# A decoder layer on one core: first slab's input first, contexts turned beside the last scan, and the triangles' products behind five of the values' eight stages

## The chip, the cores and the metric

The kernel runs on one core of a Trainium2 chip. Its engines work side by side, each with its own queue of instructions: TensorE (PE, matrix products and transposes; PEld is its weight load), VectorE (DVE), ScalarE (ACT), GpSimd (POOL) and SyncE (SP, which only issues transfers here). ACT issues transfers too, in the same queue as its activations. An engine takes its instructions strictly in the order of its queue and waits at one whose inputs are not there. The metric is the device time of one execution in microseconds (us), lower is better; it is the median of several runs.

## What is computed

One layer over x of shape (4, 1024, 256) in float32: a gated delta-rule attention, a cross attention to a context of shape (4, 77, 256), and a mixture of 8 experts (2 per token). Each is added to its input and layer-normalised. The change touches the first part and the way into the second.

```python
# attention, per head (4 heads, 64 key and 128 value channels)
normed = layernorm(x) * ln_w + ln_b
q, k, v = (causal_conv_silu(normed @ W, conv) for q, k, v)     # 4 taps
beta = sigmoid(normed @ Wb)
g = -exp(A_log) * softplus(normed @ Wa + dt_bias)
for t:                                                         # over 1024 tokens
    S = S * exp(g_t)
    v_eff = (v_t - k_t S) * beta_t
    S = S + k_t^T v_eff
    o_t = q_t S
x = layernorm(2 x + (rms(o) * norm_w * silu(normed @ Wg)) @ Wo)
# cross attention: 16 heads of 64, keys and values from the context
kh, vh = rms(ctx @ Wk), ctx @ Wv
x = layernorm(2 x + softmax(rms(x @ Wq) kh^T, masked by length) vh @ Wo)
# mixture of experts, layernorm
```

## The kernel before

**Tiling.** The 1024 tokens are cut into 8 slabs of 128, each for all 4 batch rows at once. The token-by-token recurrence is done slab by slab: within a slab the triangular system is inverted (first 32 x 32 blocks by a recurrence on DVE, then doubled on PE), between slabs the state S is carried. For one slab i the steps are generators, cut by `yield`:

- `normed(i)` (L303) loads x (L306, on SP's queue), takes the statistics (DVE L310, L311), the scale and offset rs and nm (L195 to L197, the power on POOL), and normalises on ACT (nrm, L316).
- `decays(i)` (L323) turns nrm on PE (L335), applies ln_w and ln_b on ACT (nT, L339), multiplies by Wb and Wa (pb, L352), and computes beta and the log decay g by a polynomial of some twenty small DVE steps (L366 to L388), with two Exps on ACT (L365, L376).
- `cumulated(i)` (L392) sums g over the slab by products with three triangular or full matrices (pd, L397: "the triangles' products"), takes their Exp (ex, L407; every such Exp is noted in the list `exps`) and copies parts of it on DVE (el, qw, L413 to L417).
- `project(i)` (L421) makes keys and queries: product (pp, L287), first tap on ACT (L297), three taps on DVE (L299), Silu (L442), squares (L444), and lengths (L431 to L471). `convolve` (L281) does product and taps for one of 8 channel blocks in two stages.
- `values(i)` (L474) does the same for the 4 value blocks, so 8 stages; `silus` (L478) then applies their Silu (L485), placed on ACT behind every Exp in `exps`, since Exp and Silu need different tables.
- `prepare` (L490), `blocks` (L534: the recurrence on DVE, between transfers through DRAM), `invert` (L579) and `scan` (L638) do the inversion and the recurrence itself. A scan ends with x after the attention, written to DRAM (L797).

**Order.** `interleave` (L221) steps the generators in turn, one step of each per round. For every slab one interleave runs the preparation of slab i+1, the inversion of slab i, and a chain of `decays(i+2)`, `values(i)` and `cumulated(i+2)`. Then come the Silus, and a second interleave with the scan of slab i, the recurrence of slab i+1, the projection of slab i+2 and the input of slab i+3. The start (L828 to L832) does the first slabs' steps in the same way. This written order is a priority: when the program is built, a planner fills each engine's queue from it, and an instruction that it holds to be ready can go ahead of an earlier one that is not.

**The last scan and the contexts.** Before the last scan (L854) the memory of the projection weights is given up (L845) and the cross attention's key weights are loaded into it (xwk, L853). Behind it the contexts are loaded (cx, L880), after them lens, Wv, Wo, Wq and four slabs of x, all on SP. Two zero fills (vz, L965 and L966, one on POOL, one on DVE) and one of the keys' block-diagonal tile (L894, POOL; named wdn in the profile, whose memory it uses) follow, then the contexts are turned on PE (pc, L914) and copied (cT, L917). `keys` (L919: product L924, norm with a power on POOL L939, a factor `alive` from lens L940) and `projected` (L968: values times Wv, L975, then times Wo, L1000) use cT.

**Transfers at the start.** SP's queue has the constants (sq, nw, cols, rows), then the slabs' x. ACT's queue has rw (router), rows of zeros for xd (L169) and xg (L161), Wq, Wk, Wv (L245), wba (L249), wg (L251) and wo (L253). wo is scaled by norm_w on DVE (L259). The largest of them are x (512 KB a slab), xg (1,040 KB), Wq, Wk and Wv (1,024 KB together), wg and wo (512 KB each).

Of the kernel before, what the change touches and what calls it, by code (L numbers as in the profile page):

```python
# [17 lines left out]
P = 128  # L18
# [92 lines left out]
def kernel(ctx: ExitStack, tc: tile.TileContext, a: dict, out: bass.AP):  # L111
# [18 lines left out]

    sq = const.tile([P, NSQ, P], F32, name="sq")
# [9 lines left out]
    nc.scalar.dma_start(out=rw, in_=a["rwT"].rearrange("(c p) e -> p c e", p=P))  # L141
# [19 lines left out]
    nc.scalar.dma_start(  # L161
# [7 lines left out]
    nc.scalar.dma_start(out=xd[NS * B * P :, :], in_=zero[:, 0, 0:D])  # L169

    def tokens(i, src=None):

        if src is None:
            return xd[i * B * P : (i + 1) * B * P, :].rearrange("(b p) d -> p b d", b=B)
        return src[:, i * P : (i + 1) * P, :].rearrange("b p d -> p b d")
# [59 lines left out]
    scan_scope, proj_scope = ExitStack(), ExitStack()  # L235
    wp = scan_scope.enter_context(tc.tile_pool(name="dw", bufs=1))
    wk = scan_scope.enter_context(tc.tile_pool(name="dwk", bufs=2))
    slab = scan_scope.enter_context(tc.tile_pool(name="dslab", bufs=3))
    pj = proj_scope.enter_context(tc.tile_pool(name="pj", bufs=1, side="right"))

    wqkv = pj.tile([P, KC, NCH * P], F32, name="wqkv")
    wba = pj.tile([P, KC, 2 * H], F32, name="wba")
    off = 0
    for name, n in (("L0_attn_Wq", D), ("L0_attn_Wk", D), ("L0_attn_Wv", DV)):
        nc.scalar.dma_start(  # L245
            out=wqkv[:, :, off : off + n], in_=a[name].rearrange("(c p) n -> p c n", p=P)
        )
        off += n
    nc.scalar.dma_start(out=wba, in_=a["wba"].rearrange("(c p) n -> p c n", p=P))  # L249
    wg = wp.tile([P, KC, DV], F32, name="wg")  # L250
    nc.scalar.dma_start(out=wg, in_=a["L0_attn_Wg"].rearrange("(c p) n -> p c n", p=P))  # L251
    wo = wp.tile([P, H, D], F32, name="wo")
    nc.scalar.dma_start(out=wo, in_=a["L0_attn_Wo"].rearrange("(h p) n -> p h n", p=P))  # L253

    pnw = bank("pnw")
    nc.tensor.transpose(pnw[:, 0:P], rows[:, R_NW : R_NW + HV], ident)
    nwc = wp.tile([P, 1], F32, name="nwc")
    nc.vector.tensor_scalar_mul(nwc, pnw[:, 0:1], HV**0.5)
    nc.vector.tensor_scalar_mul(  # L259
        wo.rearrange("p h n -> p (h n)"), wo.rearrange("p h n -> p (h n)"), nwc  # L260
    )


# [39 lines left out]
    def normed(i, made):  # L303

        made["x"] = xi = slab.tile([P, B, D], F32, tag="xi", name="xi", bufs=4)
        nc.sync.dma_start(out=xi, in_=tokens(i, a["x"]))  # L306
        mv = slab.tile([P, B, 2], F32, tag="mva", name="mva")
        for b in range(B):
            st = slab.tile([P, 6], F32, tag="sta", name="sta", bufs=4)
            nc.vector.bn_stats(st, xi[:, b, :])  # L310
            nc.vector.bn_aggr(mv[:, b], st)  # L311
        rs, nm = scales(slab, mv, B, "a")
        nrm = []
        for b in range(B):
            n = pj.tile([P, D], F32, tag="nrm", name="nrm", bufs=4)
            nc.scalar.activation(  # L316
                n, xi[:, b, :], AF.Identity, scale=rs[:, b : b + 1], bias=nm[:, b : b + 1]
            )
# [27 lines left out]


# [73 lines left out]
    def project(i, made):  # L421

        nT, beta, ex = made["nT"], made["beta"], made["ex"]
# [47 lines left out]
        nc.vector.scalar_tensor_tensor(cd, ex[:, 1], -1.0, nb, ALU.mult, ALU.mult)  # L471
# [380 lines left out]

    xload(xwk, "Wk")  # L853
    interleave(*scans(NS - 1))  # L854
# [24 lines left out]
    cx = cp.tile([SC, B, D], F32, name="cx", bufs=1)  # L879
    nc.sync.dma_start(out=cx, in_=a["ctx_1024"].rearrange("b s d -> s b d"))  # L880
# [28 lines left out]

    cT = cp.tile([P, KC, B * SC], F32, name="cT", bufs=1)  # L910
    for c in range(KC):
        pt = bank("pc", "pt")
        for b in range(B):
            nc.tensor.transpose(  # L914
                pt[:, b * SC : (b + 1) * SC], cx[:, b, c * P : (c + 1) * P], ident[:SC, :SC]
            )
        nc.vector.tensor_copy(cT[:, c, :], pt[:, 0 : B * SC])  # L917
# [743 lines left out]
```

## Time and profile before

| | us |
|---|---|
| three runs | 1768.39, 1771.73, 1775.53 |
| median | 1771.73 |
| the profiled execution's own time | 1777.84 |
| its span, first to last instruction | 1776.1 |
| PE busy | 1589.0 (89%) |
| DVE busy | 1177.7 (66%) |
| ACT busy | 935.8 (53%) |
| POOL busy | 565.8 (32%) |
| mean granted TensorE clock | 0.945 of full |

The profiled execution is one more run beside the three; what lies outside its span is 1.7 us. A line of the timeline gives start and duration in us, engine, line of the kernel, operation, the tile written and the tiles read, the shape, the number of instructions, and in brackets how long the engine had been idle and what ended that. The stages of the span, with the busy times of PE and DVE in each:

| stretch, us | what runs | PE busy | DVE busy |
|---|---|---|---|
| 0 to 115 | first inputs, first keys, first inversion | 53.90 | 62.76 |
| 115 to 207 | one slab: inversion, then scan | 87.51 | 68.16 |
| 207 to 298 | the next | 85.27 | 69.42 |
| 745 to 806 | last values, last scan | 52.87 | 28.03 |
| 806 to 888 | contexts, keys, values of the cross attention | 61.48 | 38.77 |
| 888 to 1330 | cross attention | 428.35 | 349.15 |
| 1330 to 1776 | experts | 403.57 | 230.58 |

### The profile page before, as it was taken

Reading aid. Unit: us, or ns where it says so; the run is one execution under the profiler, and the core shown is the slowest. Engines: PE = TensorE matmul, PEld = TensorE weight load, DVE = VectorE, ACT = ScalarE, POOL = GpSimd, SP = SyncE. Lnnn points to the kernel's source line nnn. Section 1 sums busy time; section 2 is a strip of 40 time slices with the busy share of each in tenths; the row PEclk is TensorE's granted clock in tenths of the full one; section 3 lists DMA queues with packets and bytes.
Section 4 is the critical chain, followed back from the end, with each engine's and each line's share of the span. In section 5 each row is a group of like instructions: output and inputs, shape, how many; then the busy total and the mean of one; then the engine's idle time right before and its main releaser. Section 6 shows DMA issues by size and latency. Waiting matters only on the chain. (4 is left out here: it accounts for less than half of the span.)

```text
span 1776.1 us, 28454 instructions
## 1 busy us (share of the span) xinstructions
PE 1589.0 (89%) x9524; PEld 1152.4 (65%) x9524; DVE 1177.7 (66%) x3557; ACT 935.8 (53%) x2214; POOL 565.8 (32%) x486
## 2 busy tenths in 40 slices
PE   4658999999989998985889999999989999999991
PEld 3246777676767766762657777887765666666660
DVE  4658686877777776735456888888865655555554
ACT  3425555555556454551278888888743333333333
POOL 2311312121212112014045666666733322222222
PEclk9869999898989898998999999999999999999995
DMA  4010101010101010103050011111263322332226
GB/s 142 18 19 22 39 19 43 19 43 19 43 19 30 19 31 19 25 31 132 0 190 13 22 46 43 37 49 37 94 216 67 69 45 46 46 48 46 45 33 199
DMA packets 119023, 94.20 MB, mean 53 GB/s; under 512 B 56939, under 2 KB 108639, under 8 KB 118367
## 3 DMA queue, kind: packets, MB, share of 16 engines
q1 hardware_dynamic: 100127, 69.14, 13.6%
q0 software_dynamic: 13296, 17.83, 6.0%
q10 hardware_dynamic: 5456, 5.41, 0.9%
q8 instruction: 78, 1.28, 0.3%
q14 instruction: 66, 0.54, 0.1%
HBM read 55.46 MB, written 36.90 MB: 52 GB/s over the span
## 5 line engine op out<-in xcount | busy, mean ns | idle before, releaser
L1536 POOL DMA_INDIRECT xd<-my,mrow x71 | 110.6, 1557 | 294.4 <-ACT my L1535 268.7
L1105 ACT ACTIVATE sc<-sc,ntop,rq 128x77 f32<-128x77 f32 x512 | 182.4, 448 | 5.2 <-DVE ntop L1100 4.6
L1136 PE MATMUL pxo<-ball,aT 128*128 128x256 f32 (+1 forms) x640 | 151.4, 384 | 0.8 <-DVE xs L1147 0.8
L287 PE MATMUL pp<-nT,wqkv 128*128 128x262 f32 x512 | 149.1, 430 | 0.2 <-PE pu L620 0.2
L1066 POOL TENSOR_TENSOR rq<-rq,nhalf 128x8 f32<-128x8 f32 x64 | 106.8, 1669 | 129.2 <-DVE rq L1065 128.1
L1487 PE MATMUL pgt<-wall,mxT 128*128 x284 | 134.6, 596 | 0.5 <-ACT mxT L1420 0.5
L1487 PE MATMUL pup<-wall,mxT 128*128 x284 | 134.4, 596 | 0.0
L1514 PE MATMUL pdn<-wdn,mhT 128*128 x568 | 134.2, 379 | 0.0
L759 POOL TENSOR_TENSOR so<-so,nhalf 128x4 f32<-128x4 f32 x32 | 32.6, 1018 | 312.3 <-DVE so L758 312.3
L1136 PEld LDWEIGHTS pxo<-ball,aT 128*128 128x128 f32 (+1 forms) x640 | 118.0, 192 | 15.1 <-DVE xs L1147 1.4
L1049 PE MATMUL pq<-wdn,xT 128*128 128x512 f32 x256 | 120.6, 594 | 1.5 <-ACT qsq L1059 1.0
L299 DVE SCALAR_TENSOR_TENSOR kq<-pp,cols,kq 128x256 f32<-128x256 f32 x192 | 88.3, 478 | 38.9 <-ACT kq L297 36.3
L287 PEld LDWEIGHTS pp<-nT,wqkv 128*128 128x128 f32 x512 | 99.6, 209 | 21.8 <-issue 3.3
L1514 PEld LDWEIGHTS pdn<-wdn,mhT 128*128 128x128 f32 x568 | 102.5, 190 | 11.0
L1495 DVE TENSOR_TENSOR sge<-pgt,ball 128x512 f32<-128x512 f32 x71 | 49.1, 692 | 85.3 <-PE pgt L1487 84.4
L1496 ACT ACTIVATE sge<-sge 128x512 f32<-128x512 f32 x71 | 44.7, 630 | 111.8 <-DVE sge L1495 111.8
L1487 PEld LDWEIGHTS pup<-wall,mxT 128*128 128x128 f32 x284 | 54.5, 192 | 69.0 <-issue 69.0
L1497 DVE TENSOR_TENSOR pup<-pup,ball 128x512 f32<-128x512 f32 x71 | 49.7, 699 | 69.8 <-PE pup L1487 69.7
L1114 POOL TENSOR_TENSOR sc<-sc,den 128x616 f32<-128x616 f32 x64 | 78.2, 1221 | 55.0 <-DVE den L1113 41.0
L1535 ACT ACTIVATE my<-my,mw 128x256 f32<-128x256 f32 x71 | 36.1, 508 | 106.3 <-DVE my L1534 106.3
L299 DVE SCALAR_TENSOR_TENSOR v<-pp,cols,v 128x256 f32<-128x256 f32 x192 | 81.6, 476 | 13.9 <-ACT v L297 13.2
L1085 PE MATMUL psc<-wdn,qT 128*128 128x154 f32 x512 | 78.7, 295 | 7.2 <-ACT qT L1077 7.2
(313 smaller groups left out, 3693.9 us busy)
## 6 DMA issues: line engine op xcount, KB each, us to landing
mx<-xg SPq DMA_DIRECT2D x71, 130.0 KB, 2.1
xs<-xd SPq DMA_DIRECT2D x12, 512.0 KB, 9.5
xi<-in_x SPq DMA_DIRECT2D x8, 512.0 KB, 5.1
am<-ab SPq DMA_DIRECT2D x16, 256.0 KB, 3.7
xd<-kd SPq DMA_DIRECT2D x32, 128.0 KB, 1.7
wall<-in_L_ffn_gate_w SPq DMA_DIRECT2D x8, 512.0 KB, 9.6
wall<-in_L_ffn_up_w SPq DMA_DIRECT2D x8, 512.0 KB, 8.6
xd<-xs SPq DMA_DIRECT2D x8, 512.0 KB, 4.8
```

Source lines behind the costliest of these rows:

```text
L287: mm(pp[:, 0 : 2 * (HALO + P)], lhsT=wqkv[:, kc, c * P : (c + 1) * P], rhs=nT[:, kc, 2 * j : 2 * j + 2, :].rearrange("p b t -> p (b t)"), ...
L299: nc.vector.scalar_tensor_tensor(ch, pre[:, :, n : n + P], cols[:, w0 + n : w0 + n + 1], ch, ALU.mult, ALU.add)
L1049: mm(pq, lhsT=t["xT"][:, kc, :], rhs=xwq[:, kc, c0 : c0 + HH * XD], start=kc == 0, stop=kc == KC - 1,)
L1066: nc.gpsimd.tensor_tensor(rq, rq, nhalf[:, :HH], ALU.pow)
L1085: mm(ps[:, c * 2 * SC : (c + 1) * 2 * SC], lhsT=qT[:, 2 * g + c, :], rhs=kbd[:, b, half * XC // 2 + 2 * g + c, :], start=True, stop=True,)
L1105: nc.scalar.activation(sc[:, h], sc[:, h], AF.Exp, scale=t["rq"][:, h : h + 1], bias=t["ntop"][:, h : h + 1])
L1114: nc.gpsimd.tensor_tensor(sc, sc, bc(den.unsqueeze(2), [P, HH, SC]), ALU.mult)
L1136: mm(px[:, 0:D], lhsT=aT[:w, c, :], rhs=vo[:w, b, half * NV + c, :], start=half == 0 and c == 0, stop=half == 1 and c == NV - 1,)
L1487: mm(ps, lhsT=t["xT"][:, c, :], rhs=wall[:, bass.ds(e * EW + off + c * FF, FF)], start=c == 0, stop=c == KC - 1,)
L1497: nc.vector.tensor_tensor(pu, pu, ball[:, bass.ds(e * FF + B_U, FF)], ALU.add)
L1514: mm(px[:, 0:D], lhsT=t["hT"][:, f, :], rhs=wdn[:, bass.ds(e * EV + f * D, D)], start=f == 0, stop=f == FC - 1,)
L1536: nc.gpsimd.indirect_dma_start(out=xd, out_offset=bass.IndirectOffsetOnAxis(ap=row, axis=0), in_=y, in_offset=None, compute_op=ALU.add,)
```

## The change

It has five parts.

1. x of slab 0 is loaded by the first instruction on SP's queue (`slab_of_x`), ahead of the constants. On ACT's queue only Wq, Wk, Wv and wba are left, now at its head. rw, the two fills with zeros, wg and wo move to SP's queue; wg, wo and the scaling of wo are written behind `normed(0)`.
2. `decays` has one more `yield`, between nT and the product pb.
3. At the start, `cumulated(0)` is put behind the first five stages of `project(0)` instead of ahead of it; `project` reads `ex` only where it uses it.
4. In each slab's first interleave, `cumulated(i+2)` is put behind five of the eight stages of `values(i)` instead of behind all of them.
5. The contexts' tiles cx and cT move into the pool of xwk; cx is loaded ahead of xwk, before the last scan, and the contexts are turned and copied by a third generator beside the two of the last scan.

```diff
+    def slab_of_x(i):
+        xi = slab.tile([P, B, D], F32, tag="xi", name="xi", bufs=4)
+        nc.sync.dma_start(out=xi, in_=a["x"][:, i * P : (i + 1) * P, :].rearrange("b p d -> p b d"))
+        return xi
+    x0 = slab_of_x(0)
+    wqkv = pj.tile([P, KC, NCH * P], F32, name="wqkv")
...
-    nc.scalar.dma_start(out=rw, in_=a["rwT"].rearrange("(c p) e -> p c e", p=P))
+    nc.sync.dma_start(out=rw, in_=a["rwT"].rearrange("(c p) e -> p c e", p=P))
...
-    nc.scalar.dma_start(
+    nc.sync.dma_start(
         out=xg[NE * STRIDE :, :].rearrange("(r p) d -> p r d", p=P), in_=bc(zero, [P, NE, DX])
     )
...
-    nc.scalar.dma_start(out=xd[NS * B * P :, :], in_=zero[:, 0, 0:D])
+    nc.sync.dma_start(out=xd[NS * B * P :, :], in_=zero[:, 0, 0:D])
...
-        made["x"] = xi = slab.tile([P, B, D], F32, tag="xi", name="xi", bufs=4)
-        nc.sync.dma_start(out=xi, in_=tokens(i, a["x"]))
+        made["x"] = xi = slab_of_x(i) if i else x0
...
+        yield
 
         pb = bank("pb")
...
-        nT, beta, ex = made["nT"], made["beta"], made["ex"]
+        nT, beta = made["nT"], made["beta"]
...
-        nc.vector.scalar_tensor_tensor(cd, ex[:, 1], -1.0, nb, ALU.mult, ALU.mult)
+        nc.vector.scalar_tensor_tensor(cd, made["ex"][:, 1], -1.0, nb, ALU.mult, ALU.mult)
...
     interleave(*some(normed, 0, 0))
+    wg = wp.tile([P, KC, DV], F32, name="wg")
+    nc.sync.dma_start(out=wg, in_=a["L0_attn_Wg"].rearrange("(c p) n -> p c n", p=P))
+    wo = wp.tile([P, H, D], F32, name="wo")
+    nc.sync.dma_start(out=wo, in_=a["L0_attn_Wo"].rearrange("(h p) n -> p h n", p=P))
...
-    interleave(chain(*some(cumulated, 0), *some(project, 0, 0)), *some(decays, 1, 1))
+    keys0 = project(0, made[0])
+    interleave(chain(islice(keys0, 5), *some(cumulated, 0), keys0), *some(decays, 1, 1))
...
+        vals = values(made[i])
         interleave(
             *ahead,
             *inverts(i),
-            chain(*some(decays, i + 2, i + 2), values(made[i]), *some(cumulated, i + 2)),
+            chain(*some(decays, i + 2, i + 2), islice(vals, 5), *some(cumulated, i + 2), vals),
         )
...
+    cx = xkv.tile([SC, B, D], F32, name="cx")
+    nc.sync.dma_start(out=cx, in_=a["ctx_1024"].rearrange("b s d -> s b d"))
     xload(xwk, "Wk")
-    interleave(*scans(NS - 1))
+    cT = xkv.tile([P, KC, B * SC], F32, name="cT")
+
+    def contexts():
+        for c in range(KC):
+            pt = bank("pc")
+            for b in range(B):
+                nc.tensor.transpose(
+                    pt[:, b * SC : (b + 1) * SC], cx[:, b, c * P : (c + 1) * P], ident[:SC, :SC]
+                )
+            nc.vector.tensor_copy(cT[:, c, :], pt[:, 0 : B * SC])
+            yield
+
+    interleave(*scans(NS - 1), contexts())
```

(`cx`, its load, `cT` and the same loop are taken out behind the scan.)

More of the change, by code (lines that the diff above doesn't have):

```diff
@@ L128, in new_banks @@
         ps_pool[0] = banks.enter_context(tc.tile_pool(name=name, bufs=bufs, space=PSUM, **kw))
+    scan_scope, proj_scope = ExitStack(), ExitStack()
+    wp = scan_scope.enter_context(tc.tile_pool(name="dw", bufs=1))
+    wk = scan_scope.enter_context(tc.tile_pool(name="dwk", bufs=2))
+    slab = scan_scope.enter_context(tc.tile_pool(name="dslab", bufs=3))
+    pj = proj_scope.enter_context(tc.tile_pool(name="pj", bufs=1, side="right"))
+    def slab_of_x(i):
[4 more added lines that the diff above has]
+    wqkv = pj.tile([P, KC, NCH * P], F32, name="wqkv")
+    wba = pj.tile([P, KC, 2 * H], F32, name="wba")
+    off = 0
+    for name, n in (("L0_attn_Wq", D), ("L0_attn_Wk", D), ("L0_attn_Wv", DV)):
+        nc.scalar.dma_start(
+            out=wqkv[:, :, off : off + n], in_=a[name].rearrange("(c p) n -> p c n", p=P)
+        )
+        off += n
+    nc.scalar.dma_start(out=wba, in_=a["wba"].rearrange("(c p) n -> p c n", p=P))
     sq = const.tile([P, NSQ, P], F32, name="sq")
@@ L168, with tokens @@
     xd = tc.dram_tile([NS * B * P + P, D], F32, name="xd")
-    nc.scalar.dma_start(out=xd[NS * B * P :, :], in_=zero[:, 0, 0:D])
[L171 to L175, printed above, removed]
+    nc.sync.dma_start(out=xd[NS * B * P :, :], in_=zero[:, 0, 0:D])
+    def tokens(i):
+        return xd[i * B * P : (i + 1) * B * P, :].rearrange("(b p) d -> p b d", b=B)
     def rsqrt(pool, src, n, eps, scale, name):
@@ L227, in interleave @@
                     gens.remove(g)
[L235 to L261, printed above, removed]
     nega = pj.tile([P, H], F32, name="nega")
@@ L828 @@
     interleave(*some(normed, 0, 0))
+    wg = wp.tile([P, KC, DV], F32, name="wg")
+    nc.sync.dma_start(out=wg, in_=a["L0_attn_Wg"].rearrange("(c p) n -> p c n", p=P))
+    wo = wp.tile([P, H, D], F32, name="wo")
+    nc.sync.dma_start(out=wo, in_=a["L0_attn_Wo"].rearrange("(h p) n -> p h n", p=P))
+    pnw = bank("pnw")
+    nc.tensor.transpose(pnw[:, 0:P], rows[:, R_NW : R_NW + HV], ident)
+    nwc = wp.tile([P, 1], F32, name="nwc")
+    nc.vector.tensor_scalar_mul(nwc, pnw[:, 0:1], HV**0.5)
+    nc.vector.tensor_scalar_mul(
+        wo.rearrange("p h n -> p (h n)"), wo.rearrange("p h n -> p (h n)"), nwc
+    )
     interleave(*some(decays, 0, 0), *some(normed, 1, 1))
-    interleave(chain(*some(cumulated, 0), *some(project, 0, 0)), *some(decays, 1, 1))
+    keys0 = project(0, made[0])
+    interleave(chain(islice(keys0, 5), *some(cumulated, 0), keys0), *some(decays, 1, 1))
     interleave(*prepares(0), *some(cumulated, 1), *some(normed, 2, 2))
@@ L851, in xload @@
         nc.sync.dma_start(out=w, in_=a[f"L0_xattn_{n}"].rearrange("(c p) n -> p c n", p=P))
+    cx = xkv.tile([SC, B, D], F32, name="cx")
+    nc.sync.dma_start(out=cx, in_=a["ctx_1024"].rearrange("b s d -> s b d"))
     xload(xwk, "Wk")
-    interleave(*scans(NS - 1))
+    cT = xkv.tile([P, KC, B * SC], F32, name="cT")
[5 more added lines that the diff above has]
+                    pt[:, b * SC : (b + 1) * SC], cx[:, b, c * P : (c + 1) * P], ident[:SC, :SC]
+                )
+            nc.vector.tensor_copy(cT[:, c, :], pt[:, 0 : B * SC])
+            yield
+    interleave(*scans(NS - 1), contexts())
     scan_scope.close()
@@ L878 @@
     xwo = cp.tile([P, XC, D], F32, name="xwo", bufs=1)
-    cx = cp.tile([SC, B, D], F32, name="cx", bufs=1)
-    nc.sync.dma_start(out=cx, in_=a["ctx_1024"].rearrange("b s d -> s b d"))
     leni = xk.tile([P, B], I32, name="leni")
@@ L908 @@
     nc.vector.tensor_tensor(wqk, cols[:, C_XQ : C_XQ + 1], cols[:, C_XK : C_XK + 1], ALU.mult)
[L910 to L917, printed above, removed]
     def keys(b):
```

## The prediction

> **What bounds the kernel now.** I read the page's slices first: PE is busy 89% of the span, but the low slices are the first three and slices 19 and 20, the only places where the change moves much. Three questions follow: what starts PE, what PE waits for between two slabs, and what stands between the last scan and the cross attention. Times below are us from the span's start.
>
> The timeline of the first 45 us (start, duration, engine, line; in brackets the idle time before and what ended it):
>
> ```profile
> 10.61 0.75 DVE L310 BATCH_NORM_STATS2 sta<-xi 128x6 f32<-128x256 f32 x2 [3.80 <-DMA xi<-in_x]
> 13.93 0.15 DVE L195 TENSOR_SCALAR rs<-mva 128x4 f32<-128x4 f32 x1
> 13.98 1.28 ACT L265 ACT_TABLE_LOAD   x1 [13.98 <-DMA xi<-in_x]
> 18.02 0.23 DVE L197 SCALAR_TENSOR_TENSOR nm<-mva,rs 128x4 f32<-128x4 f32 x2
> 18.21 4.04 ACT L316 ACTIVATE nrm<-xi,nm,rs 128x256 f32<-128x256 f32 x8 [2.73 <-DVE nm L197]
> 22.97 3.82 PE L352 MATMUL pb<-wba,nT 128*128 128x8 f32 x16 [1.95 <-ACT nT L339]
> 31.15 1.46 PE L397 MATMUL pd<-g,sq 128*128 128x16 f32 x6 [4.36 <-DVE g L388]
> 33.34 1.95 PE L287 MATMUL pp<-nT,wqkv 128*128 128x262 f32 x4
> 35.84 1.52 DVE L299 SCALAR_TENSOR_TENSOR kq<-pp,cols,kq 128x256 f32<-128x256 f32 x3 [2.16 <-ACT kq L297]
> ```
>
> Slab 0's input lands at 10.6. Its scale (rs, 13.93) is followed by its offset (nm) only at 18.02, because DVE has the statistics of slabs 1 and 2 in between and waits for their inputs. Then the key products (L287) stand behind the triangles' product (L397), which waits 4.36 for the polynomial of g. From there one chain runs to the first inversion, and the waits show that PE has nothing else meanwhile:
>
> ```profile
> PE pw L587 <- DMA tt<-ub: 24.3, 1, 24.3
> ```
>
> So what starts this chain earlier starts everything earlier.
>
> Between the last scan and the keys, timeline again:
>
> ```profile
> 806.83 0.70 SPq L880 DMA_DIRECT2D cx<-in_ctx  x1
> 811.14 1.26 PE L914 MATMUL pc<-sq,cx 77*128 77x77 f32 x8 [7.90 <-DMA cx<-in_ctx]
> 814.73 5.34 PE L924 MATMUL pkv<-xwk,cT 128*77 128x512 f32 x8 [2.32 <-DVE cT L917]
> 820.02 1.64 POOL L939 TENSOR_TENSOR kr<-kr,nhalf 77x8 f32<-77x8 f32 x1 [6.70 <-DVE kr L938]
> ```
>
> PE ends the scan at 803.24, waits 7.90 for the contexts and 2.32 for their copies.
>
> Between two slabs (slab 2's values to its scan), ACT and PE:
>
> ```profile
> 324.52 1.28 ACT L485 ACT_TABLE_LOAD   x1
> 326.50 0.40 PE L650 MATMUL pv<-sq,v 128*128 128x128 f32 x1 [1.76 <-ACT v L485]
> 330.40 0.47 ACT L297 ACTIVATE kq<-pp,cols 128x256 f32<-128x256 f32 x1 [2.92 <-PE pp L287]
> 330.78 0.62 ACT L485 ACTIVATE v<-v 128x512 f32<-128x512 f32 x1
> 331.45 0.44 PE L650 MATMUL pv<-sq,v 128*128 128x128 f32 x2 [1.08 <-ACT v L485]
> ```
>
> The Exp of L407 (324.29) has to precede the Silu table and v's Silus. But DVE's 18 convolution steps end only at 328.45 (321.32 + 7.13), so the last Silu cannot come earlier than that.
>
> **The change, part by part.**
>
> *Input first.* x0 is SP's first issue (0.73). The row of four xi loads has 6.3 to 11.5 from issue to landing, the 320 KB of sq 3.4; x0 lands between 0.73 + 3.4 = 4.1 and 7.0, I take 5.5. Statistics 1.75 (10.61 to 12.36), rs 0.15, the power on POOL 1.05, nm 0.2, gaps 0.4: nrm starts at 9.0 against 18.21. Only four nrm now stand before nT (2.0 of the 4.04), so nT ends near 12.7 against 23.58, and pb near 16.5. ACT hid nothing before: its first work (13.98) came just after its last DMA issue (13.58 + 0.37). With five issues fewer it is free by 7.8 (wba's issue, 7.39 + 0.4). Those five (rw, 1,040 KB of xg, xd, wg, wo) go to SP, some 0.45 each = 2.3, all ahead of x1. Bytes ahead of x1's end: 3.7 MB without xg, 5.0 with it; at the 0.37 MB/us of 4 to 20 us, after first bytes at 2.3, x1 lands at 12.4 to 15.8 (before: 13.6). Its statistics and offset take 3.5, so slab 1's transposes, which PE has in order behind the first key product, can run at 16 to 19.5. That costs 0 to 1.1 there and is covered by DVE's backlog. The scaling of wo (0.74, DVE) is now written ahead of slab 1; if it stands before nm of slab 0 it holds the chain until wo lands, some 6.
>
> *Key products before the triangles.* They follow pb at 16.5 instead of 33.34, DVE's steps 2.5 later at 19. Before, these ran 35.84 to 50.37 = 14.5, slab 1's polynomial included. Now slab 0's polynomial (21 steps of 0.17, 3.5), slab 2's statistics (1.75) and el/qw (0.8) share DVE: 20.6, end 39.6 against 50.37, a gain of 10.8. The Exp of slab 0 and the Silus of its keys now mix on ACT: I count two more table loads. The row prices one at 1.28 and the next activation starts 1.31 after the one before (48.87 to 50.18), so 2.6 in all; as ACT has slack in part, I take 1. Start: **-10**; ends -14.5 (no sharing) and -4 (wo in front).
>
> [...]
>
> *Contexts beside the last scan.* Eight transposes (1.26 on PE) and two copies (0.85 on DVE) go into a scan where PE waits anyway (1.91 at 758.31). cx goes out before xwk, whose issue at 754.44 waited 13.7 for PE's last key/value product; with cx's 4.3 (806.83 to 811.1) it lands at 758.7, about when PE asks. Cost 0, at most 1.3 + 1. The keys' first product can then start at 804 to 806.4 instead of 814.73. What is late next is POOL: two memsets end at 813.33 (809.12 + 4.21), and the first power (820.02) can come no earlier than 813.4; alive (813.62 on DVE) is due there too. So 820.02 - 813.4 = 6.6, the rest of the section follows this chain until PE fills at 856. I take **-6**; ends -10.7 (all PE idle) and -3 (xwv, landing near 812 to 816, holds the values' products).
>
> *Triangles behind five stages; a yield before pb.* pd moves ahead of three stages (0.74 of PE, neutral), Exp and Silu table (1.5) into ACT's gaps of 0.41 to 2.53. The 1.76 wait goes, but DVE ends at 328.45 as before, and el/qw (0.75) now stand before its last steps. Per slab, six slabs: -2 (1.76 plus part of the 2.3 that the last Silu stood behind kq) to +0.75. As DVE decides, I take -0.5: **-3**, ends -12 and +4.5.
>
> Sum: -10 - 6 - 3 = -19. Span 1776.1 gives 1757; the profiled run itself took 1777.84, 1.7 more, and the median 1771.73 is 6.1 below that: 1777.8 - 19 - 6.1 = **1753**.
>
> **Rivals.**
> *B, the gains are taken back at once*: wo's scaling or slab 1's input holds the start (-4), the memsets and xwv the keys (-2 to -3), the slabs give 0. Sum -6: 1766. For it: 2.3 of issues and 1.5 MB more before x1 on SP. Against: DVE has nm ready before wo can land, if it is placed so.
>
> *C, slower: PE waits for g.* pb is now written one round later, behind L629. PE's order in the trace is the written one (pk, pu, pb, pl, pp). If it stays so, PE's gap before pl grows from 2.0 (304.11) to 4, and g, from za at 304.4 to 317.72, comes 5.3 later, 323. pd then stands at PE's head from 320.8 (323.52 less three stages of 0.9), with three stages and all the scan's products queued behind: 2.2. The stretch after the present gap shows what idling does besides:
>
> ```profile
> 304.00:310.00 6.00, 5.89 (x37) 5.33 (x38) 2.56 (x13) 2.24 (x6) 1.80 (x2) 0.50 0.00 0
> ```
>
> (after the length stand five engines' busy times, then the granted clock: 0.50). L629 took 3.67 against 2.04 at 672.76, L500 behind it 3.55 against 1.88 at 293.08: 3.3 for the gap of today. For one twice as long I add between nothing and 2.3; with the 2.2 that is up to 4.5 a slab, six slabs 27, less 16 from the rest: 1772 + 11 = 1783. It decides from 2.7 a slab on. Against: pb is ready while PE is idle there, so it need not stay behind.
>
> [...] This trace shows 0.50 after 2.0 already.
>
> *D, ACT decides between the slabs*: both waits (1.76, 1.08) and the 0.88 before L671 go, -2.5 a slab: -15 instead of -3, 1741.
>
> *That it does nothing* would need the x0 issue and the cx issue to stay where they are; both are first in their queue by the text.
>
> **Chances.** Forecast 0.55 (own range 1741 to 1763), B 0.20, C 0.12, D 0.13. With three runs from 1768 to 1776, about 0.5% (9 us) can be told from no change. Faster by more: 0.51 + 0.13 + 0.06 of B = 0.70; within: 0.18; slower: 0.12. The range 1735 to 1775 takes in D's half, the forecast and B, and leaves out C.
>
> **What would show it.** Right: nrm near 9, first L287 near 17, pw L587 near 98 instead of 108.5; PE's pkv at 804 to 807 and kr near 813.4 counted from the scan's end; pd before the last three stages with no wait above 0.5. Wrong: L259 waiting for wo before L197; PE pd waiting for g in each slab; clock 0.5 stretches longer than now; v's last step more than 12 after the first of bp's second eight (317.80 to 328.45 now).

## The result and the profile after

Five runs of the changed kernel took 1781.55, 1789.19, 1789.68, 1791.23 and 1793.37 us, median **1789.68**; five of the kernel before had a median of 1772.98. The ratio is 1.0086, 95% interval 1.006 to 1.0112: slower by 0.9%, where 1753 was forecast with a range up to 1775. The profiled execution is the lowest of the five (1781.55, span 1779.8, granted clock 0.942); the other four had clocks of 0.931 to 0.934.

Read stage by stage in the two profiled executions:

| stretch | before | after | difference |
|---|---|---|---|
| start to the first pw (first inversion) | 108.5 | 101.5 | -7.0 |
| first pw to the last slab's pw | 628.6 | 639.5 | +10.9 |
| last slab's pw to the end of the last scan's px | 66.1 | 68.3 | +2.2 |
| end of the last scan to the first query product | 84.4 | 80.6 | -3.8 |
| from there to the end | 888.5 | 889.9 | +1.4 |

The rows add up to +3.7, and the medians differ by 16.7: the profiled execution before lies 4.9 above its median, the one after 8.1 below. The other runs left no trace, so where the ones after lost their further time is not shown.

The start and the handoff gained, as forecast, though less. The slabs lost as much as these two gained, even in this quickest of the five executions.

**Slabs.** PE's waits (what for; us in total, times, longest us), before, then after:

```profile
PE pl L629 <- DVE tr L623: 8.5, 5, 2.1
```

```profile
PE pl L623 <- DVE tr L617: 20.8, 7, 4.0
PE pv L644 <- ACT v L479: 13.7, 16, 1.7
```

and PE's timeline in slab 3, before (first pw at 384.7) and after (first pw at 379.9):

```profile
397.13 2.73 PE L629 MATMUL pl<-tr,bp 64*64 64x64 f32 x32 [1.66 <-DVE tr L623]
399.79 2.11 PE L287 MATMUL pp<-nT,wqkv 128*128 128x262 f32 x4
```

```profile
392.32 3.64 PE L623 MATMUL pl<-tr,bp 64*64 64x64 f32 x32 [3.51 <-DVE tr L617]
395.89 3.58 PE L346 MATMUL pb<-wba,nT 128*128 128x8 f32 x16
...
399.32 3.76 PE L494 MATMUL pe<-ee,sq 128*128 128x512 f32 x4
403.01 3.67 PE L628 MATMUL pu<-tt,wt 64*64 64x64 f32 x32
406.62 2.11 PE L281 MATMUL pp<-nT,wqkv 128*128 128x262 f32 x4
408.66 3.54 PE L508 MATMUL pk<-kq 64*128 64x256 f32 x16
412.13 3.80 PE L281 MATMUL pp<-nT,wqkv 128*128 128x262 f32 x16
```

pb now stands behind pl, in the place that pp had, so PE has nothing for 3.51 us ahead of pl. Then it works at half speed from pl through pk: pb takes 3.58 (1.95 with the clock full), pu 3.67 (2.08), pk 3.54 (2.00). The same in the windows of this slab (length; busy us of PE, PEld, DVE, ACT and POOL with instructions; then granted clock, DMA share, GB/s):

```profile
379.90:389.90 10.00, 8.90 (x205) 6.94 (x203) 6.44 (x22) 6.78 (x11) 3.46 (x4) 1.00 0.27 80
389.90:399.90 10.00, 7.58 (x49) 7.40 (x50) 4.15 (x13) 2.28 (x6) 3.09 (x3) 0.57 0.01 2
399.90:409.90 10.00, 10.00 (x46) 6.41 (x46) 6.20 (x20) 3.52 (x8) 2.54 (x2) 0.50 0.00 0
409.90:419.90 10.00, 9.79 (x50) 7.88 (x48) 9.47 (x31) 4.45 (x9) 2.08 (x2) 0.90 0.24 33
```

The third line is the one to read: PE is busy all of it, at half clock. A look at busy shares alone would call that stretch perfect.

**Start.** DVE after:

```profile
10.14 0.16 DVE L220 SCALAR_TENSOR_TENSOR nm<-mva,rs 128x4 f32<-128x4 f32 x1
16.88 0.75 DVE L832 TENSOR_SCALAR wo<-wo,nwc 128x1024 f32<-128x1024 f32 x1 [6.59 <-DMA wo<-in_L_attn_Wo]
18.31 0.75 DVE L303 BATCH_NORM_STATS2 sta<-xi 128x6 f32<-128x256 f32 x2 [0.68 <-DMA xi<-in_x]
...
42.53 0.48 DVE L293 SCALAR_TENSOR_TENSOR kq<-pp,cols,kq 128x256 f32<-128x256 f32 x1
```

nm of slab 0 is out at 10.14 in place of 18.02, ahead of the scaling of wo, as forecast. DVE then waits 6.59 for wo, and slab 1's input comes at 18.3 (expected 12.4 to 15.8). The last line is DVE's last convolution step of slab 0's keys: it ends at 43.0, where 39.6 was forecast and 50.4 measured before. From there on the chain is about as long as it was, and the first pw comes 7.0 earlier. ACT loads tables at 30.23, 32.17 and 34.32, where Exp and Silu of two slabs now mix; up to the first pw it has eight loads, six before, which are the two more that were counted.

**Last scan and handoff**, after, PE first (the ACT line between stands beside the first stop):

```profile
762.09 0.46 PE L872 MATMUL pc<-sq,cx 77*128 77x77 f32 x4 [1.86 <-DMA cx<-in_ctx]
...
765.45 0.78 PE L872 MATMUL pc<-sq,cx 77*128 77x77 f32 x4
766.80 1.44 PE L692 MATMUL py<-vt,tt 128*128 128x128 f32 x5 [0.57 <-DVE cT L875]
```

```profile
761.46 0.63 ACT L479 ACTIVATE v<-v 128x512 f32<-128x512 f32 x1 [1.72 <-DVE v L293]
```

```profile
810.13 3.66 PE L937 MATMUL pkv<-xwk,cT 128*77 128x512 f32 x8 [0.81 <-DVE kd L784]
818.50 2.39 PE L988 MATMUL pvt<-cT,xwv 128*128 128x308 f32 x4 [4.71 <-DMA xwv<-in_L_xattn_Wv]
```

The handoff on POOL and on DVE:

```profile
815.21 4.21 POOL L916 MEMSET wdn<- 128x4928 f32 x1
820.52 3.25 POOL L952 TENSOR_TENSOR kr<-kr,nhalf 77x8 f32<-77x8 f32 x2 [1.11 <-DVE kr L951]
```

```profile
815.89 3.54 DVE L921 CAST lens<-leni 128x4 f32<-128x4 int32 x1
815.90 3.53 DVE L949 TENSOR_REDUCE ks<-ksq 77x8 f32<-77x512 f32 x1
```

In the last scan PE's queue stops 1.86 at pc, put down to cx. This stop isn't new: the values that the next product (pv) needs come from ACT at 762.09 as well (761.46 + 0.63), and before PE waited 1.91 for them at the same place. New are the transposes themselves, 0.57 for their copy ahead of py, and a longer spell at half clock behind them: 6.83 us, 3.41 before. The keys' first product starts 0.8 after the scan and not 11.5, but 7 of these 10.7 us are given back: a cast of 512 numbers takes 3.54 and a sum 3.53 (the next sum takes 0.68), both ending with POOL's fill. The first power comes at 820.52, which is 11.2 behind the scan's end (16.8 before), and POOL takes the second power ahead of the first product with `alive`.

### The profile page after: what moved, and what is told of

Its sections match the earlier page's. It is cut to its first block, busy times and chain, and to the rows that moved or that the text cites. A ratio compares the mean times of both kernels' runs of the same rounds, so it can differ in the third digit from the quotient of the medians.

```text
span 1779.8 us, 28453 instructions
## 1 busy us (share of the span) xinstructions
PE 1597.8 (90%) x9524; PEld 1155.6 (65%) x9524; DVE 1177.8 (66%) x3557; ACT 937.3 (53%) x2216; POOL 565.7 (32%) x486
## 5 line engine op out<-in xcount | busy, mean ns | idle before, releaser
L281 PE MATMUL pp<-nT,wqkv 128*128 128x262 f32 x512 | 139.9, 410 | 0.3 <-PE pu L614 0.2
L1149 PEld LDWEIGHTS pxo<-ball,aT 128*128 128x128 f32 (+1 forms) x640 | 118.1, 193 | 15.8 <-DVE xs L1160 2.1
L281 PEld LDWEIGHTS pp<-nT,wqkv 128*128 128x128 f32 x512 | 94.5, 198 | 21.6 <-issue 5.1
L293 DVE SCALAR_TENSOR_TENSOR kq<-pp,cols,kq 128x256 f32<-128x256 f32 x192 | 88.5, 480 | 25.5 <-ACT kq L291 24.1
```

Source lines behind the costliest of these rows:

```text
L281: mm(pp[:, 0 : 2 * (HALO + P)], lhsT=wqkv[:, kc, c * P : (c + 1) * P], rhs=nT[:, kc, 2 * j : 2 * j + 2, :].rearrange("p b t -> p (b t)"), ...
L293: nc.vector.scalar_tensor_tensor(ch, pre[:, :, n : n + P], cols[:, w0 + n : w0 + n + 1], ch, ALU.mult, ALU.add)
L1149: mm(px[:, 0:D], lhsT=aT[:w, c, :], rhs=vo[:w, b, half * NV + c, :], start=half == 0 and c == 0, stop=half == 1 and c == NV - 1,)
```

## The experiments

The theories: **T1**, the extra stage of `decays` puts pb behind pl, and PE's idling with the half clock after it costs the slabs (later cut into T1a, the idling as such, and T1b, the later chain of g on DVE); **T2**, the triangles' products behind five stages cost it; **T3**, the transfers on SP or the contexts do. A fourth came up on the way: **T4**, the clock goes by how wide the products are that stand about pl.

### One part undone or alone

`e1_no_yield`: the change without the `yield` between nT and pb.

```diff
-        yield
 
         pb = bank("pb")
```

> The whole change but for its second part: nT and pb stand in one stage of decays again. T1 (the extra stage puts pb behind the products pl, PE then idles up to 4.0 us ahead of pl where it idled 2.1, and the half clock that follows costs the slabs their time): pb is back ahead of pl in PE's queue, PE's longest wait for tr is 2.1 again (20.8 us of waits in all becomes 8 to 9), and the time is 1757 to 1766, below before. T2 (the triangles' products behind five stages cost the slabs their time): 1784 to 1792, as with the whole change. T3 (the transfers moved to SP and the contexts in the last scan cost it): 1784 to 1792 too.

Measured: 1757.89, ratio to before 0.9886 (0.9859 to 0.9913). Waits for tr 8.0.

`e2_no_triangles`: the change with the order of before for `cumulated`.

```diff
-            chain(*some(decays, i + 2, i + 2), islice(vals, 5), *some(cumulated, i + 2), vals),
+            chain(*some(decays, i + 2, i + 2), vals, *some(cumulated, i + 2)),
```

> The whole change but for its fourth part: cumulated stands behind all eight stages of values again. T1: PE still idles 3.5 to 4.0 ahead of pl; the time stays at 1784 to 1794. T2: the slabs are as before, and start and handoff keep their gain of 7.0 + 3.8 - 2.2 = 8.6: 1760 to 1767. T3: 1784 to 1792.

Measured: 1793.15, 1.0087 (1.0061 to 1.0112). The whole change has 1.0086: beside the stage, the triangles' move is worth next to nothing.

`e3_yield_alone`: the kernel before with the `yield`.

```diff
+        yield
         pb = bank("pb")
```

> The kernel before with the second part alone, the stage between nT and pb. T1: PE's longest wait for tr grows from 2.1 to 3 to 4 us, the stretch from the first pw to the last grows by 10 to 20, and the time is 1783 to 1797. T2 and T3: within 4 us of before, 1769 to 1777.

Measured: 1800.35, 1.0134 (1.0107 to 1.016), above T1's 1783 to 1797. Waits for tr 21.0, longest 4.0.

`e4_triangles_alone`: the kernel before with `cumulated` behind five of the eight stages.

```diff
-            chain(*some(decays, i + 2, i + 2), values(made[i]), *some(cumulated, i + 2)),
+            chain(*some(decays, i + 2, i + 2), islice(vals, 5), *some(cumulated, i + 2), vals),
```

> The kernel before with the fourth part alone, cumulated behind five of the eight stages. T1: waits for tr as before (8.5 us in all), the time within 5 us of before, 1767 to 1777. T2: 1783 to 1797, the loss being in the inversions of slabs 3 and 4 above all. T3: within 4 us of before.

Measured: 1759.76, 0.9905 (0.9878 to 0.9932), below what any theory had.

T2 and T3 are out. The one line `yield` costs 22.8 us alone (1800.35 against 1777.59) and 31.8 within the change (1789.68 against 1757.89; the kernel before took 1772.98 beside the one and 1777.59 beside the other, so by the ratios it is 35). T1 had no room for the other half of the result: the triangles' move, without the stage, gains 17.8, and it was priced at 3.

Where it goes is read from one window over six slabs, first pw to seventh pw, in which each kernel has the same 4092 or 4093 products (e6, e8, e9 and e10 have some added). Before, e4, e5 (below: the stage at the start only) and after:

```profile
108.50:659.60 551.10, 517.22 (x4092) 391.72 (x4093) 412.20 (x1366) 308.10 (x714) 114.35 (x110) 0.92 0.13 28
```

```profile
108.20:640.50 532.30, 503.42 (x4093) 381.37 (x4094) 410.90 (x1366) 306.72 (x714) 114.35 (x110) 0.95 0.13 28
```

```profile
103.30:636.20 532.90, 503.88 (x4092) 380.76 (x4093) 411.76 (x1366) 306.79 (x714) 114.28 (x110) 0.95 0.13 29
```

```profile
101.50:664.00 562.50, 522.14 (x4093) 394.74 (x4094) 416.17 (x1366) 306.64 (x714) 114.40 (x110) 0.92 0.12 27
```

The same products keep PE busy for 503.4, 503.9, 517.2 or 522.1 us. That difference is the clock. Adding up the trace's records of the granted clock gives the time at half clock, and an account that holds for all runs: busy time less half of the half-clock time is 473 to 481 where no product is added.

| kernel | six slabs | PE not busy | PE busy | at half clock |
|---|---|---|---|---|
| before | 551.1 | 33.9 | 517.2 | 85.0 |
| e1, no stage | 532.4 | 29.4 | 503.0 | 50.5 |
| e2, triangles as before | 573.0 | 39.4 | 533.7 | 121.9 |
| e3, stage alone | 568.2 | 41.7 | 526.5 | 105.8 |
| e4, triangles alone | 532.3 | 28.9 | 503.4 | 50.4 |
| e5, stage at the start only | 532.9 | 29.0 | 503.9 | 50.9 |
| after | 562.5 | 40.4 | 522.1 | 88.5 |
| e6, unread pb ahead too | 564.1 | 28.0 | 536.1 | 95.0 |
| e7, x1 and x2 first | 533.5 | 27.9 | 505.6 | 55.1 |
| e8, pb twice ahead | 535.3 | 22.1 | 513.2 | 47.2 |
| e9, wide behind pb | 574.7 | 38.7 | 536.1 | 102.4 |
| e10, wide ahead of pb | 532.7 | 26.7 | 506.0 | 34.4 |
| e11, pp ahead of pb | 550.5 | 37.6 | 512.9 | 64.8 |
| e12, pp beside pb | 547.2 | 32.7 | 514.5 | 68.2 |
| e13, as e12 in the slabs | 539.3 | 33.1 | 506.2 | 50.7 |
| e14, as e5 in the slabs | 532.4 | 28.6 | 503.8 | 51.2 |

So from e5 to after the slabs lose 29.6: 11.4 idle and 18.2 clock. From before to e4 they gain 18.8: 5.0 idle and 13.8 clock. That clock is gained at the head of the scan, where PE waits for v: spells of half clock that begin more than 25 us behind a slab's first pw add up to 41.0 us before and to 10.2 in e4. In slab 3 PE waits there 1.76, 1.08 and 0.88 before, and in e4 once:

```profile
414.48 0.44 PE L650 MATMUL pv<-sq,v 128*128 128x128 f32 x2 [1.58 <-ACT v L485]
```

### Where the stage helps

`e5_yield_start_only`: the stage for slabs 0 and 1 alone.

```diff
-        yield
-
+        if i < 2:
+            yield
         pb = bank("pb")
```

> The whole change, with the extra stage of decays for slabs 0 and 1 only. T1 (in the slabs the stage costs time, at the start it helps: the first inversion began at 101.5 with it and at 107.3 without): first pw at 101 to 102, the slabs as without the stage (611 from the first pw to the last), 1749 to 1755. If the stage's place at the start only moved a table load that is paid elsewhere: 1756 to 1760, as without it.

Measured: 1754.84, 0.9888 (0.9864 to 0.9912); first pw at 103.3, six slabs as in e1. The upper end of what was expected: its start is 4.0 better than e1's 107.3, the time 3.1, and by the ratios nothing (0.9888 and 0.9886), so a gain in time from the stage at the start is not shown. Against before the start gains 5.2 here and 7.0 in the whole change, with the same code there.

`e7_x1_x2_first`: e5, and the inputs of slabs 1 and 2 ahead of rw, xg, xd, wg and wo on SP, wo's scaling later.

```diff
+    ahead_x = {0: x0, 1: slab_of_x(1), 2: slab_of_x(2)}
     rw = const.tile([P, KC, NE], F32, name="rw")
...
-    wg = wp.tile([P, KC, DV], F32, name="wg")
...
+    wg = wp.tile([P, KC, DV], F32, name="wg")
...
     interleave(blocks(0, made[0]), *some(project, 1, 1))
```

> As the whole change with the stage for slabs 0 and 1 only, and the inputs of slabs 1 and 2 loaded straight behind the constants, wg, wo and the scaling of wo written behind the preparation of slab 0. If the start is held by slab 1's input, which came at 18.3 behind 2.6 MB on SP's queue, and by DVE's wait for wo: x1 is there at 13 to 15, the first pw comes at 95 to 99, and the time is 3 to 6 below the same kernel without this. If DVE's own backlog holds it: pw within 1.5 of 101.5 and the same time.

Measured: 1758.65, 0.9906 (0.9884 to 0.9927), first pw at 104.9. Missed. DVE's wait for wo is gone and slab 1's statistics are early, but they and slab 2's now stand ahead of slab 0's offset, as in the kernel before. DVE, then ACT:

```profile
14.39 0.23 DVE L221 SCALAR_TENSOR_TENSOR nm<-mva,rs 128x4 f32<-128x4 f32 x2
```

```profile
14.58 4.04 ACT L310 ACTIVATE nrm<-xi,nm,rs 128x256 f32<-128x256 f32 x8 [4.95 <-DVE nm L221]
```

So nm of slab 0 comes at 14.39 (10.36 in e5) and the first key product at 19.78 (14.47), 5.3 later, while the first pw is only 1.6 later than in e5. The run undoes one gain while it makes another, and so it does not show whether the 6.59 us and slab 1's 18.3 were on the path. That stays open.

### Is it the idling?

`e6_pb_twice_behind`: the change, with the product of pb made a first time ahead of the stage, unread.

```diff
+        if i >= 2:
+            pw = bank("pbx")
+            for b in range(B):
+                for kc in range(KC):
+                    mm(pw[:, b * 2 * H : (b + 1) * 2 * H], lhsT=nT[:, kc, b, HALO:], rhs=wba[:, kc, :], ...)
         yield
 
         pb = bank("pb")
```

> The whole change, and for slabs 2 to 7 the product of pb is made once more ahead of the extra stage, into a bank that nothing reads: PE has 1.95 us more of work a slab where it idles ahead of pl, while the pb that g is made from stays behind pl, as in the whole change. T1a (what costs is PE idling 4 us and the half clock after it): waits for tr 8 to 10 us in all, the granted clock 0.945 or more, 1762 to 1772: six slabs pay 1.95 each for the product that stands outside the gap, and no more. T1b (what costs is that g's chain on DVE runs later): 1783 to 1793, no better than the whole change or worse.

Measured: 1784.79, 1.0046 (1.0028 to 1.0063). T1a falls as it was put: the idle time is that of e5 (28.0 against 29.0), the waits for tr 8.4, and yet 95.0 us run at half clock. The time lies in T1b's range; e11 below speaks against T1b. Its slab 3, PE:

```profile
392.28 3.67 PE L634 MATMUL pl<-tr,bp 64*64 64x64 f32 x32 [1.49 <-DVE tr L628]
395.88 3.58 PE L357 MATMUL pb<-wba,nT 128*128 128x8 f32 x16
399.31 3.76 PE L505 MATMUL pe<-ee,sq 128*128 128x512 f32 x4
403.00 3.67 PE L639 MATMUL pu<-tt,wt 64*64 64x64 f32 x32
```

The same stretch of e5, with a gap about as long:

```profile
384.72 2.41 PE L623 MATMUL pl<-tr,bp 64*64 64x64 f32 x32 [1.31 <-DVE tr L617]
387.06 2.11 PE L281 MATMUL pp<-nT,wqkv 128*128 128x262 f32 x4
388.97 2.25 PE L494 MATMUL pe<-ee,sq 128*128 128x512 f32 x4
391.15 2.08 PE L628 MATMUL pu<-tt,wt 64*64 64x64 f32 x32
```

In e5 pp and pe, 262 and 512 columns wide, stand side by side and the clock comes back within pe. In e6 pb, 8 columns wide, stands in pp's place; pe alone is followed by pu, and the half clock goes on for 20.5 us. That is T4.

`e8_pb_twice_ahead`: e5 with the unread pb ahead of the read one, both ahead of pl.

```diff
+        if i >= 2:
+            pw = bank("pbx")
+            ...
         if i < 2:
             yield
         pb = bank("pb")
```

> As the whole change with the stage for slabs 0 and 1 only, and for slabs 2 to 7 the product of pb made twice, both ahead of pl, the first unread: 1.95 us of useless work a slab in the gap ahead of pl that is 1.0 to 2.0 long. T1a (the idling is paid by a half clock behind it): PE's waits for tr nearly 0, the granted clock higher, and the time 4 to 15 below the same kernel without the useless product. T1b, or a clock that doesn't mind gaps under 2 us: 0 to 6 above it.

Measured: 1760.2, 0.9916 (0.9893 to 0.9939): T1a's 4 to 15 below e5 missed, 5.4 above, as the other expectation had it. Two windows of its slab 3 (from its first pw at 371.5) show why:

```profile
371.50:381.50 10.00, 10.00 (x215) 8.07 (x214) 6.60 (x22) 6.77 (x11) 3.48 (x4) 1.00 0.27 82
381.50:391.50 10.00, 10.00 (x64) 7.70 (x63) 6.87 (x26) 4.06 (x10) 3.24 (x4) 0.68 0.00 0
```

PE is busy for all 20 us, and the clock falls all the same, at 385.0. The products of the 5.8 us ahead of the fall have 8 to 64 columns.

### Is it the width?

`e10_wide_ahead_pl`: e5 with two unread products of 128x512 where e8 has the unread pb, the same time of PE.

```diff
+        if i >= 2:
+            pw = bank("pbx")
+            for n in range(2):
+                mm(pw, lhsT=ident, rhs=sq[:, 0:4, :].rearrange("p n t -> p (n t)"), start=True, stop=True)
         if i < 2:
             yield
         pb = bank("pb")
```

> As the whole change with the extra stage for slabs 0 and 1 only, and for slabs 2 to 7 two wide products (128x512, unread) ahead of pb, where the run with pb made twice had a narrow one of the same 1.95 us. T4 (the clock goes by how wide the products are, not only by whether PE is busy): the clock stays over 0.9 through pl, which then takes 1.3 in place of 2.7, and the time is 1738 to 1752. If wide and narrow are the same to the clock: 1755 to 1763, as with pb twice.

Measured: 1755.58, 0.9897 (0.9871 to 0.9923): the time is that of the second expectation. The clock did what T4 says: from 51 to 34 us at half speed, and none about pl in any of the six slabs. Slab 3, from its first pw at 369.1:

```profile
379.10:389.10 10.00, 10.00 (x94) 7.95 (x93) 7.58 (x25) 5.56 (x13) 4.92 (x5) 1.00 0.01 2
```

The time did not: the two products cost 1.9 a slab, and six of these (11.4) are about what the clock (half of 16.5) and the filled gap (2.3) give back. The 1738 to 1752 was worked out without them.

`e9_wide_behind_pb`: the change with the two wide products between pb and pe.

```diff
                     stop=kc == KC - 1,
                 )
+        if i >= 2:
+            pw = bank("pbx")
+            for n in range(2):
+                mm(pw, lhsT=ident, rhs=sq[:, 0:4, :].rearrange("p n t -> p (n t)"), start=True, stop=True)
         yield
```

> The whole change, and for slabs 2 to 7 two products of 128x512 behind pb, into a bank that nothing reads: useless work between pb and pe. T4 (the half clock that sets in about pl ends only after a stretch of wide products; before, pp and pe stood there side by side, 5.5 us at half speed; in the whole change pe stands alone between the narrow pb and pu, 3.8 us, and the half clock lasts some 20 us): the clock is full again by the second pu, products from pk on are at full speed, and the time falls although there is more to do: 1768 to 1781. T1b (g's chain being late is what costs): the extra work is added, 1790 to 1802.

Measured: 1793.79, 1.012 (1.0095 to 1.0145). A miss for T4; the time is in T1b's range. The spell about pl ended earlier where it had been 20.5 (10.2 in slab 3, 13.65 in slab 4), but was no shorter elsewhere, and in five slabs a second one stands at the scan's first products, some 44 after the slab's first pw, so that there is more half clock in all, 102.4.

`e11_pp_ahead_of_pb`: the change with the first stage of values ahead of pb, nothing added.

```diff
+        dec = iter(decays(i + 2, made[i + 2]) if i + 2 < NS else ())
...
-            chain(*some(decays, i + 2, i + 2), islice(vals, 5), *some(cumulated, i + 2), vals),
+            chain(islice(dec, 3), islice(vals, 1), dec, islice(vals, 4), *some(cumulated, i + 2), vals),
```

> The whole change, and in each slab the first key-value stage is put ahead of pb: PE has pl, pp, pe, pu, pb, pk; pb and with it g's chain are some 7 us later still than in the whole change, and no work is added. T4 (pp and pe side by side again end the half clock): 1753 to 1768. T1a (PE has no pb for the gap ahead of pl and idles 3.5 to 4.0): 1780 to 1792. T1b (g's chain late): 1790 or more.

Measured: 1773.91, 1.0005 (0.9987 to 1.0024), between the expectations. PE in slab 3:

```profile
392.54 3.40 PE L623 MATMUL pl<-tr,bp 64*64 64x64 f32 x32 [3.46 <-DVE tr L617]
395.88 2.11 PE L281 MATMUL pp<-nT,wqkv 128*128 128x262 f32 x4
397.78 2.82 PE L494 MATMUL pe<-ee,sq 128*128 128x512 f32 x4
400.53 2.08 PE L628 MATMUL pu<-tt,wt 64*64 64x64 f32 x32
...
412.59 0.81 PE L391 MATMUL pd<-g,sq 128*128 128x16 f32 x6 [2.45 <-DVE g L382]
```

With pp beside pe again the clock is back before pu, in each slab after 6.8 us or less; T1b is out as the main cause, since g is later still and the time 16 lower than after. What stays is the gap of 3.46 and, now, pd waiting 2.45 for g.

`e12_pp_beside_pb`: e5 with the first stage of values in the round of pb, so that useful wide products fill the gap.

```diff
+    def both(*gens):
+        for g in gens:
+            next(g, None)
+        yield
...
+            chain(islice(dec, 2), both(dec, vals), dec, islice(vals, 4), *some(cumulated, i + 2), vals),
```

> As the whole change with the extra stage for slabs 0 and 1 only, and in each slab the first stage of values (two wide products) in the same round as pb: PE has pb, pp, pl, pp, pe. No work is added. By the account (479 of PE's work for six slabs at the full clock, plus idle time, plus half of the time at half clock): waits for tr fall from 8.8 to 1 to 3, the half clock in six slabs from 51 to 20 to 40, so six slabs take 515 to 527 in place of 533, and the time is 1738 to 1751. If the clock's loss doesn't go with what stands ahead of pl: half clock 45 to 55, six slabs 527 to 533, 1750 to 1757.

Measured: 1766.41, 0.9953 (0.9939 to 0.9966). A miss. The waits for tr went, or nearly (3.5 in 3 waits), but pd, now one stage earlier, waits 1.2 to 1.5 for g in four slabs, and 68.2 us run at half clock. The same slab code in e13 has slabs 3 and 4 of one execution at 88.0 and 93.0, with 3.4 and 13.7 us at half clock. So the order of the products does not alone settle the spells.

What does can be read from all sixteen traces together. Within a trace, every change of the clock lies on one grid of 3.413 us, to within 2 ns. For each window of this grid, add up the columns of PE's product records (the traces have two for a float32 product: 16 for the 8 products of pb), each weighted with the rows of the array that it uses, so that 64 of 128 count half; a window at full clock has some 3800 in the median. In the six slabs, all 275 windows with less than 1540 were followed by a window at half clock, though PE was busy for 99% or more of the time in 140 of them. Of the 2290 others, 2249 were followed by full clock and 41 by half. The figure 1540 was chosen on these traces, and the 41 stay unexplained.

Slab 3 shows it. The window ahead of pl's spell has 591 after, 816 in e5 and 662 in e8; in e10 it has 1926, and no spell follows. In the changed kernel's spell the windows have 695, 410, 1272, 1370, 1395 and 1865, and then the clock is full. Where the grid cuts matters too: in e13 no window about pl has less than 1669 in slab 3, and one has 1220 in slab 4, with the same code. So T4 holds in a wider form, for these traces: the half clock goes with few columns and rows worked off in a window, not with the time that PE is busy.

### The handoff and the last scan

`e13_fills_out_of_the_way`: e12 with lens loaded before the last scan, the keys' tile filled on ACT, the two other fills written behind the first product of the values.

```diff
+    leni = xkv.tile([P, B], I32, name="leni")
+    nc.sync.dma_start(out=leni, in_=a["lens"])
...
-    nc.gpsimd.memset(kbd, 0.0)
...
+            if j == 0:
+                nc.scalar.copy(kbd[:, b], bc(zero[:, :, 0:1], [P, XC, 2 * SC]))
...
-    nc.gpsimd.memset(vz[0], 0.0)
-    nc.vector.memset(vz[1], 0.0)
...
+                if half == 0 and p == 0:
+                    nc.gpsimd.memset(vz[0], 0.0)
+                    nc.vector.memset(vz[1], 0.0)
```

> As the run before it, and in the handoff: the lengths loaded before the last scan, the zero fill of the keys' block-diagonal tile in four parts on ACT (each behind the first square of its batch row) in place of one on POOL, and the two other fills behind the first product of the values. Read from the end of the last scan to the first query product (81 before this edit). If the fills hold DVE and POOL: the cast and the first sum take 0.7 and not 3.5, the first kr comes 4 to 7 after the scan's end in place of 11 to 14, and the stretch takes 74 to 79. If Wv's landing and PE's own work hold it: 80 to 82, and the same time as the run before it.

Measured: 1768.53, 0.9966 (0.9953 to 0.9979); scan to query 77.7 against 81.6 in e12, inside 74 to 79, the time no lower: its seven runs go from 1758.62 at a clock of 0.951 to 1769.15 at 0.945. The cast still took 2.79: the planner put POOL's other fill ahead of the keys' powers, as POOL was free.

`e14_fills_tied_behind_keys`: e5 with the same edits, the two fills tied behind the first power and the first norms, and each copy of `contexts` four rounds later.

```diff
+            yield from [None] * 4
             pt = bank("pc")
...
+                if half == 0 and p == 0:
+                    with tc.issue_after(first["kr"].ins):
+                        nc.gpsimd.memset(vz[0], 0.0)
+                    with tc.issue_after(first["kn"].ins):
+                        nc.vector.memset(vz[1], 0.0)
```

> As the whole change with the extra stage for slabs 0 and 1 only (1754.8 measured; its last scan, first pw to last px, 68.6; scan's end to first query 80.7), with the lengths loaded before the last scan, the keys' tile filled in four parts on ACT, the two other fills tied behind the first power (POOL) and the first norms (DVE) of the keys, and each copy of contexts four rounds later. If the fills hold the keys: cast and first sums at 0.7, the first kr ends 5 to 8 after the scan's end in place of 12, scan to query 74 to 78. If Wv's landing holds it: 79 to 81. Contexts: if their place in PE's queue cost the last scan 2.2, it takes 66 to 67 again; if what they add is work that PE has no room for, 68 to 69. The time: 1746 to 1752, or 1753 to 1757 if neither holds.

Measured: **1749.2**, 0.9842 (0.9818 to 0.9867), the best of all. Last scan 66.4 (68.6 in e5), scan to query 76.2 (80.7). DVE and POOL, the scan's end being at 779.9:

```profile
783.05 0.17 DVE L921 CAST lens<-leni 128x4 f32<-128x4 int32 x1 [0.67 <-ACT kd L790]
...
784.07 0.67 DVE L953 TENSOR_REDUCE ks<-ksq 77x8 f32<-77x512 f32 x1
...
790.92 0.69 DVE L959 TENSOR_TENSOR kn<-pkv,kr 77x512 f32<-77x512 f32 x1 [2.19 <-POOL kr L957]
```

```profile
786.91 0.31 POOL L957 TENSOR_SCALAR kr<-kr,alive 77x8 f32<-77x8 f32 x1
...
790.83 2.74 POOL L1002 MEMSET vz<- 128x3176 f32 x1
```

The cast is back at 0.17 and the sum at 0.67, the first kr is done 7.3 after the scan's end, and the norm kn takes its 0.69 beside POOL's fill. Both causes are shown: the fills held the keys (the early lengths and the tile's move to ACT were changed with them and are not told apart), and the place of pc in PE's queue cost the last scan its 2.2. Most of the 2.2 is clock again: the same 577 records keep PE busy for 61.97 us in e5 and 60.35 in e14, with one window of 3.41 more at half clock in e5. e9, which has pc at the old place but one window only, took 66.9.

## Why the prediction was wrong

- **Start, -10:** measured -7.0. x0 landed at 5.54 (5.5 taken), nm came at 10.14 ahead of wo as argued, the first pp at 14.25 (17). The order of events was right. The term that was mis-sized is DVE's work: its convolution for slab 0 was to end at 39.6 and ended at 43.0. Its first step came at 21.59 and not at 19, behind slab 1's statistics, whose input landed at 18.3 and not at 12.4 to 15.8; that this is the reason was not tested by itself (e7 changes slab 0's offset with it).
- **Contexts, -6 and 0:** measured -3.8 and +2.2. Right in what comes early (the keys' product 0.8 after the scan) and in naming the memsets, but the powers were taken to follow POOL's fill at once. The fill also held DVE's cast (3.54 beside it, 0.17 in e14 without it), and DVE's sums behind it: the first power came 11.2 behind the scan's end (10.2 by the forecast), and the first norm kn gained 4.1 of the 6, as POOL took a second power first. The last scan's cost of 0 to 1.3 + 1 was priced at the lower bound; that 2.2 is near the upper one is luck, since most of it is a term that the bound did not have, the clock.
- **Triangles, -3:** measured -17.8 alone. The row looked at was DVE's last step, which "decides". Rival D, ACT's waits going, worth -15, had the place right: the waits at the scan's head did shrink. But only 5.0 of the 18.8 in six slabs is idle time; 13.8 is PE doing the same products at a higher clock, which D did not have. Beside the stage the gain was not there (e2 has 1.0087, the change 1.0086).
- **The stage ahead of pb, 0:** this is the step that failed. "pb is ready while PE is idle there, so it need not stay behind" was the argument against rival C. The planner left it behind in every slab: PE's waits for tr rose from 8.5 to 20.8, and this one line cost 31.8. Rival C had the place, the wider gap and the half clock behind it, and a time of 1783; it was given 0.12. In its price, the wait of pd for g (2.2) did not come, the clock (0 to 2.3 a slab) was 3.0 (18.2 over six), and the gap itself, 1.9 a slab (11.4 over six), was not counted. Its 1783 fell 7 short, and that near by luck, since it took 16 off for the rest, where start, handoff and last scan gave 8.6. It put the half clock down to the idling ahead of pl; in e8 the gap is filled with a narrow product and the clock falls all the same, at 385.0, with PE busy for 10.00 of 10 us (over six slabs 47.2 us at half clock, 50.9 in e5).
- **What was no part of any rival:** that the triangles' move pulls at the clock too, against the stage. Rival C had the clock for the stage alone, and at most at 2.3 a slab.

The time predicted, 1753, is met by the change without that stage in the slabs (1754.84), but that is luck: other terms than the forecast's make it up, less from start and contexts, far more from the triangles.

## What to carry to other kernels

Where PE is busy nine tenths of the time, compare the busy time of the same number of instructions in two profiles, and not the idle gaps alone: here the same 4093 products took 503.4 us in e4 and 522.1 in the changed kernel, and the difference is the clock (50.4 and 88.5 us at half). Here a stretch of small products cost the clock as idling did: in e8 it fell at 385.0 with PE busy for 10.00 of 10 us, in the changed kernel it fell in a gap of 3.51. An extra stage in a written order is not free because its work could go early; take the written order as what will happen, and price each instruction that then leaves a gap and each that takes a wide product's place. Zero fills and casts near a handoff like this one, where a cast took 3.54 us beside POOL's fill and 0.17 without it, belong behind the chain that everything waits for, and a planner needs to be told so.

## What the runs showed of the hardware

- The half clock comes in spells of 3.41, 6.83, 10.24, 13.65, 17.07 and 20.48 us in the slabs: whole multiples of 3.41, in all sixteen profiles, but for the last spell, which runs into the kernel's end.
- In e8 the clock fell while PE was busy for 20 us, after 5.8 us of products of 8 to 64 columns, and with wide products in the same place (e10) it did not. What it went with in these traces is the columns worked off in a window of 3.413 us, weighted with the rows used: all 275 windows under 1540 were followed by half clock, 140 of them with PE busy for 99% or more. Above 1540, 41 of 2290 were too, and these stay open.
- In the changed kernel a fill on POOL that writes 4928 columns (815.21 to 819.42) stood beside a cast of 4 columns on DVE, which took 3.54 us and ended at 819.43; in e14, without a fill beside it, the cast took 0.17. The sum shown with 3.53 stood behind the cast (0.67 in e14). In e14 kn stood beside a fill of 2.74 and took 0.69, as it did at 787.25 with no fill beside it.
